# A mask add on GpSimd, split from one instruction of 1024 columns into two of 512

## The chip, the core and the metric

The kernel runs on one core of a Trainium2 chip. The metric is device time in microseconds (us) from launch to end, over repeated runs; smaller is better. A separate profiled execution gives the trace that all readings here come from. Engine names: PE is the matrix engine, DVE the vector engine, ACT the scalar engine, POOL is GpSimd, SP the engine that issues the DMAs.

## The reference, cut to what matters

The input is 64 graphs of 256 nodes with 512 features each, an adjacency matrix per graph and a node mask. Four layers follow each other; each normalises the rows (layer norm, then maximum with zero), runs a graph layer and adds its result to `x`. The change lies in layer 1, an attention over neighbours with 8 heads:

```python
dense = e_self[..., :, None] + e_neigh[..., None, :]
dense = jax.nn.leaky_relu(dense, negative_slope=0.2)
dense = dense + NEG_BIG * (1.0 - A[:, None, :, :])
att = jax.nn.softmax(dense, axis=-1)
```

The third line is the neighbour mask: -1e10 is added wherever two nodes aren't joined. Layers 0 and 3 weigh nodes by a softmax over one number per node, layer 2 uses `tanh` of masked scores.

## The kernel before, in words

**Tiling.** A graph's rows lie on 128 partitions, two rows to a partition (`NC` = 2). All data is float32. Buffers come from pools of one size each: `big` (1024 columns), `mid` (512 columns), `bank` (PSUM, 512 columns).

**Order.** Each graph is a set of named steps. A table of times (`TIMES`, with other tables for the first and the last graphs) says when each step of each graph is due; `Plan.run` sorts all steps of all 64 graphs by due time and records their instructions in that order. Every instruction is tied to the one before it on its engine, so the order on each engine is fixed, and an engine never overtakes a waiting instruction. Several graphs are in flight at once: while graph b is in layer 1, graph b+1 is in layer 0 and older graphs are in layers 2 and 3. DMAs are all issued by SP, in order.

**The steps around the change.** Heads are handled in four pairs p = 0 to 3, each in one `big` tile `e{p}` of 2 heads x 2 x 256 columns:

- `ea{p}` (line 1445, ACT): four Prelu instructions of 256 columns, two per head, fill the tile.
- `eg{p}` (line 1452, POOL): the mask `negt` (512 columns, the same for both heads) is added to the whole tile.
- `eb{p}` (line 1458, DVE): the row maximum is subtracted.
- `ex{p}` (line 1464, ACT): exponential. `po{p}` (line 1476, PE): product with the features. `eh{p}` (line 1487, POOL): sum of the two column halves.

On POOL, in the steady part of the run, the order of one turn of the loop is: `add3` of an old graph (line 1722, two instructions), `eg2`, `eg3`, the four sums of a Strassen-like product (`xsa` and `xsb`, lines 1172, 1173, 1179, 1180, which read rows brought by a gather DMA of line 1017), `eg0`, then a normalisation (lines 1092, 1097, 1098), `eg1`, and further sums, normalisations and `eh` steps.

On DVE, in the same stretch: sixteen max reductions (line 1407), then `mxv`, four small instructions of 128x16 (lines 1418, 1420, 1421, 1422) that turn the row maxima into the value to subtract, `mxt` (line 1427), then for the next graph the scores of layer 0 (`s0v`, line 1312), transposes and the softmax (line 1136), four scaled additions (`add0`, line 1325) and the sum of the row sums (`ms1`, line 1333). PE waits for `s0v` at its transposes of line 1131. ACT waits for `ms1` at line 1082, POOL then computes the scale (lines 1092 to 1098), ACT normalises (line 1103), and after that comes the first exponential (line 1464) for which PE waits at line 1476.

Of the kernel before, what the change touches and what calls it, by code (L numbers as in the profile page):

```python
# [11 lines left out]
OP = mybir.AluOpType  # L12
# [4 lines left out]
P = 128  # L17
D = 512
KC = D // P
N = 256  # L20
NC = N // P
# [705 lines left out]
class Graph:  # L727
# [5 lines left out]
    def step(self, name):  # L733
        def add(run):
            self.steps[name] = run
            return run
        return add
# [21 lines left out]
def tile_four_gnn_layers(ctx: ExitStack, tc: tile.TileContext, x, adj, nodemask,  # L759
# [6 lines left out]
    nc = tc.nc  # L766
# [253 lines left out]
    def graph(b):  # L1020

        g = Graph(plan)
# [415 lines left out]
        def attention(p):  # L1438
            @step(f"ea{p}")
            def _():  # L1440
                e = g.take("pair", 2, name=f"e{p}")
                for s in range(2):
                    h = 2 * p + s
                    for j in range(NC):
                        nc.scalar.activation(e[:, s, j, :], g[f"s{h // HA}"][:, h % HA, :], AF.Prelu,  # L1445
                                             bias=st["ec"][:, j, H + h:H + h + 1], alpha=0.2)
                g.done(f"s{p // 2}")

            @step(f"eg{p}")
            def _():  # L1450
                e = g[f"e{p}"]
                nc.gpsimd.tensor_tensor(e, e, g["negt"][:, None].to_broadcast([P, 2, NC, N]), OP.add)  # L1452
                g.done("negt")

            @step(f"eb{p}")
            def _():
                e = g[f"e{p}"]
                nc.vector.tensor_tensor(e, e, g[f"m{p // 2}"][:, p % 2 * 2:p % 2 * 2 + 2, None, :].to_broadcast([P, 2, NC, N]),  # L1458
                                        OP.subtract)
                g.done(f"m{p // 2}")  # L1460

            @step(f"ex{p}")
            def _():
                nc.scalar.activation(g[f"e{p}"], g[f"e{p}"], AF.Exp)  # L1464


            @step(f"po{p}")
            def _():
                e, q = g[f"e{p}"], p // 2
                if p % 2 == 0:  # L1470
                    g.take("bank", name=f"o{q}")
                po = g[f"o{q}"].rearrange("p (r n) -> p r n", r=2)
                for j in range(NC):
                    for s in range(2):
                        h = 2 * p + s
                        nc.tensor.matmul(po[s * U:(s + 1) * U, p % 2, :],  # L1476
                                         g[f"feats{j}"][:, E + h * U:E + (h + 1) * U],
                                         e[:, s, j, :], start=(j == 0), stop=(j == NC - 1))
                g.done(f"e{p}")
                for j in range(NC):  # L1480
                    g.done(f"feats{j}")


            @step(f"eh{p}")
            def _():
                e = g[f"e{p}"]
                nc.gpsimd.tensor_tensor(g.take("half", name=f"h{p}"), e[:, :, 0, :], e[:, :, 1, :], OP.add)  # L1487
                g.done(f"e{p}")
# [273 lines left out]
```

## Time and profile before

| what | us |
|---|---|
| median of 3 runs (lowest, highest) | 3696.07 (3695.48, 3696.09) |
| profiled execution, its own time | 3695.02 |
| its span, first to last instruction | 3693.2 |
| PE busy | 3401.5 (92%) |
| DVE busy | 3314.2 (90%) |
| ACT busy | 2781.7 (75%) |
| POOL busy | 2270.6 (61%) |
| POOL, line 1452: 256 instructions, mean 2.370 | 604.0 |
| POOL idle just before line 1452 | 98.6 |

A line of the profile names the source line, the engine, the operation, what is written and read, the shape and the count; behind the bar stand the busy time, the mean length of one instruction in ns, and the idle time of the engine just before it with what ended it. A line of the timeline starts with the time from the start of the span and the length, both in us; square brackets hold the idle time before it. Consecutive equal instructions are merged ("x2").

### The profile page before, as it was taken

The page shows a single profiled execution, that of the slowest core. Times are in us where ns is not written, and L with a number is a line of the kernel's source. Part 1 is how long each engine was busy: PE and PEld are TensorE (multiplying, and loading weights), DVE is VectorE, ACT ScalarE, POOL GpSimd, SP SyncE. Part 2 cuts the span into 40 slices and gives each one's busy share as a digit, 9 for nine tenths or more (in the row PEclk, how much of TensorE's full clock was granted, in tenths as well). Part 3 has the DMA queues.
Part 4 walks back from the last instruction along what each step waited for, and adds up shares of the span by engine and source line. Part 5 has one row for each costly group of instructions (what it writes and reads, how often), then busy time and mean ns, then how long its engine had stood idle before and what let it go on. Part 6 is the DMA issues. An engine that isn't in the chain of part 4 may idle for free.

```text
span 3693.2 us, 61427 instructions
## 1 busy us (share of the span) xinstructions
PE 3401.5 (92%) x16834; PEld 2175.5 (59%) x16834; DVE 3314.2 (90%) x8248; ACT 2781.7 (75%) x6533; POOL 2270.6 (61%) x2452
## 2 busy tenths in 40 slices
PE   5688999999999999999999999999999999989988
PEld 3455655665665666666666666666666666556554
DVE  6789998999999999999999989999989999999985
ACT  3667777787787787787778778778878778778765
POOL 3565665666666666666666666666666666565653
PEclk8799999999999999999999999999999999999999
DMA  6666766777777777777777777777777777767663
GB/s 185 181 188 208 207 213 212 222 220 216 222 219 218 222 222 217 225 224 224 227 215 221 226 216 217 230 222 219 226 216 219 223 219 221 217 204 216 197 190 119
DMA packets 995143, 785.28 MB, mean 213 GB/s; under 512 B 791984, under 2 KB 862192, under 8 KB 994800
## 3 DMA queue, kind: packets, MB, share of 16 engines
q1 hardware_dynamic: 994800, 781.35, 70.3%
q8 instruction: 137, 2.24, 0.2%
q14 instruction: 206, 1.69, 0.1%
HBM read 511.12 MB, written 270.01 MB: 212 GB/s over the span
## 4 chain that ended last, share of the span: by engine, by line
POOL 22%; DVE 18%; issue 15%; PE 14%; DMA 12%; ACT 7%; SPq 6%; POOLq 0%; ACTq 0%; DVEq 0%
PE bank L1188 9%; DMA big<-sq_d 8%; SPq L1017 5%; DVE big L1458 4%; DVE junk L1407 3%; POOL big L1452 3%; POOL rstd L1092 3%; POOL mid L1487 3%; POOL big L1173 3%; DMA sq_d<-big 3%; POOL big L1172 2%; POOL big L1179 2%; DVE big L1202 2%; DVE big L1012 2%; ACT big L1082 2%
## 5 line engine op out<-in xcount | busy, mean ns | idle before, releaser
L1188 PE MATMUL bank<-t_s,big 128*128 128x264 f32 (+3 forms) x3072 | 978.0, 452 | 8.3 <-DVE big L1657 6.1
L1188 PE MATMUL bank<-w_s,big 128*128 128x264 f32 (+2 forms) x3072 | 850.9, 410 | 45.9 <-DMA big<-sq_d 36.3
L1188 PEld LDWEIGHTS bank<-t_s,big 128*128 128x128 f32 x3072 | 583.0, 194 | 306.5 <-issue 180.5
L1188 PEld LDWEIGHTS bank<-w_s,big 128*128 128x128 f32 x3072 | 583.8, 196 | 278.5 <-issue 131.8
L1452 POOL TENSOR_TENSOR big<-big,mid 128x1024 f32<-128x1024 f32 x256 | 604.0, 2370 | 98.6 <-ACT big L1445 89.0
L1012 DVE STREAM_TRANSPOSE big<-big 128x512 f32<-128x512 f32 x640 | 483.6, 782 | 143.6 <-ACT big L1103 143.5
L1092 POOL TENSOR_TENSOR rstd<-rstd,power 128x2 f32<-128x2 f32 x256 | 183.9, 718 | 678.8 <-ACT rstd L1088 628.2
L1103 ACT ACTIVATE big<-big,shift,rstd 128x512 f32<-128x512 f32 x512 | 387.7, 805 | 167.3 <-POOL shift L1098 167.0
L1172 POOL TENSOR_TENSOR big<-big 128x256 f32<-128x256 f32 x256 | 226.6, 885 | 412.9 <-DMA big<-sq_d 278.7
L1487 POOL TENSOR_TENSOR mid<-big 128x512 f32<-128x512 f32 x256 | 377.1, 1493 | 138.2 <-ACT big L1464 138.2
L1407 DVE CUSTOM_DVE_ANT_0 junk<-big,bank 128x256 f32<-128x256 f32 x1024 | 428.9, 419 | 35.3 <-DMA big<-er_d 4.1
L1082 ACT ACTIVATE big<-big,sum 128x512 f32<-128x512 f32 x512 | 363.8, 712 | 116.7 <-DVE sum L1333 83.7
L1445 ACT ACTIVATE big<-big,ec 128x256 f32<-128x256 f32 x1024 | 428.8, 496 | 5.4 <-DMA big<-er_d 3.1
L1202 DVE TENSOR_TENSOR big<-bank,big 128x320 f32<-128x320 f32 (+1 forms) x704 | 399.5, 571 | 18.2 <-PE bank L1188 13.7
L1476 PE MATMUL bank<-big,big 128*64 128x256 f32 x2048 | 260.7, 388 | 92.2 <-ACT big L1464 91.9
L1458 DVE TENSOR_TENSOR big<-big,big 128x1024 f32<-128x1024 f32 x256 | 325.2, 1309 | 6.5 <-DMA big<-m_d 6.5
L1633 PE MATMUL bank<-big,big 64*128 64x256 f32 x2048 | 283.8, 398 | 50.5 <-DVE mx L1407 31.4
L1657 DVE TENSOR_TENSOR big<-bank,mid 128x512 f32<-128x512 f32 x512 | 319.9, 677 | 5.3 <-PE bank L1633 5.2
L1664 ACT ACTIVATE big<-big 128x512 f32<-128x512 f32 x512 | 293.1, 619 | 14.3 <-DVE big L1657 12.3
L1464 ACT ACTIVATE big<-big 128x1024 f32<-128x1024 f32 x256 | 267.8, 1052 | 41.4 <-DVE big L1458 33.6
L1633 PEld LDWEIGHTS bank<-big,big 64*128 64x128 f32 x2048 | 219.7, 197 | 131.4 <-ACT big L1621 65.1
L1536 ACT ACTIVATE big<-big,rs 128x64 f32<-128x64 f32 x1024 | 257.4, 334 | 24.5 <-DVE rs L1525 13.2
(132 smaller groups left out, 5877.8 us busy)
## 6 DMA issues: line engine op xcount, KB each, us to landing
sq_d<-big SPq DMA_DIRECT2D x448, 512.0 KB
big<-sq_d SPq DMA_DIRECT2D x1792, 128.0 KB
big<-er_d SPq DMA_DIRECT2D x256, 512.0 KB
big<-m_d SPq DMA_DIRECT2D x128, 512.0 KB
big<-in_x_dram SPq DMA_DIRECT2D x64, 512.0 KB
out_dram<-big SPq DMA_DIRECT2D x64, 512.0 KB
mid<-in_adj_dram SPq DMA_DIRECT2D x64, 256.0 KB
mid<-in_adj_dram SPq DMA_DIRECT2D x256, 64.0 KB
```

The costliest lines, as they stand in the source:

```text
L1012: nc.vector.transpose(sq.rearrange("p (r k i c) -> p c k r i", r=4, k=KC, c=NC)[:, c], t[:, c])
L1082: nc.scalar.activation(g["hn"][:, c, :], g["xt"][:, c, :], AF.Square, scale=-float(D), bias=st["sum"][:, c:c + 1], accum_out=st["ssq"][:, ...
L1103: nc.scalar.activation(g["hn"][:, c, :], g["xt"][:, c, :], AF.Relu, bias=st["shift"][:, c:c + 1], scale=st["rstd"][:, c:c + 1])
L1188: nc.tensor.matmul(p, a()[:, k], w[:, k], start=(k == 0), stop=(k == 1))
L1202: nc.vector.tensor_tensor(out(), g[i][:, :w], old(), OP.add)
L1407: nc.vector.tensor_tensor_reduce(junk, g[f"n{h // HA}"][:, h % HA, :], g["far"][:, c * N:(c + 1) * N], 1.0, -BIG, OP.add, OP.max, g["mx"][ ...
L1445: nc.scalar.activation(e[:, s, j, :], g[f"s{h // HA}"][:, h % HA, :], AF.Prelu, bias=st["ec"][:, j, H + h:H + h + 1], alpha=0.2)
L1452: nc.gpsimd.tensor_tensor(e, e, g["negt"][:, None].to_broadcast([P, 2, NC, N]), OP.add)
L1458: nc.vector.tensor_tensor(e, e, g[f"m{p // 2}"][:, p % 2 * 2:p % 2 * 2 + 2, None, :].to_broadcast([P, 2, NC, N]), OP.subtract)
L1487: nc.gpsimd.tensor_tensor(g.take("half", name=f"h{p}"), e[:, :, 0, :], e[:, :, 1, :], OP.add)
L1633: nc.tensor.matmul(ps[s][:, m, :], chunk(g["xpt"][half, p], m), g["xc"][half, p, :], start=True, stop=True)
L1657: nc.vector.tensor_tensor(th[:, s], g[f"ps{p}{s}"].rearrange("p (m n) -> p m n", m=NC), g["at"], OP.mult)
```

## The change

`eg{p}` loops over the two heads of a pair and adds the mask to each head's 512 columns in an instruction of its own. The broadcast of the mask over the heads goes away, since each instruction reads the mask once. The order of the steps, the other engines' instructions and all buffers stay as they are.

```diff
             @step(f"eg{p}")
             def _():
                 e = g[f"e{p}"]
-                nc.gpsimd.tensor_tensor(e, e, g["negt"][:, None].to_broadcast([P, 2, NC, N]), OP.add)
+                for s in range(2):
+                    nc.gpsimd.tensor_tensor(e[:, s], e[:, s], g["negt"], OP.add)
                 g.done("negt")
```

## The prediction

> **What bounds the kernel.** I first read busy shares: PE 92%, DVE 90%, POOL only 61%. So POOL's work matters only through what it makes others wait for. Next, PE's waits in the steady part (697 to 3115 us, 44 turns of the loop, one graph leaving per turn; mean turn 54.95 us):
>
> ```profile
> PE bank L1476 <- ACT big L1464: 60.1, 44, 2.5
> PE bank L1131 <- DVE bank L1312: 39.8, 43, 2.0
> PE bank L1633 <- DVE mx L1407: 24.6, 44, 1.0
> ```
>
> These 124 us (2.8 us per turn) are nearly all of PE's idle time there. Two of three end on DVE, so I read DVE's timeline in one turn, then POOL's over the same microseconds:
>
> ```profile
> 1853.06 0.92 DVE L1418 TENSOR_TENSOR mx<-mx,ec 128x16 f32<-128x16 f32 x1
> 1854.02 0.83 DVE L1420 TENSOR_SCALAR mx<-mx 128x16 f32<-128x16 f32 x1
> 1854.88 0.17 DVE L1421 SCALAR_TENSOR_TENSOR mx<-mx 128x16 f32<-128x16 f32 x1
> 1855.09 0.59 DVE L1422 TENSOR_TENSOR mx<-mx 128x16 f32<-128x16 f32 x1
> ...
> 1855.88 0.20 DVE L1312 SCALAR_TENSOR_TENSOR bank<-bank,big 128x64 f32<-128x64 f32 x1
> ```
>
> ```profile
> 1845.90 2.51 POOL L1722 TENSOR_TENSOR big<-big,big 128x512 f32<-128x512 f32 x2
> 1849.28 4.68 POOL L1452 TENSOR_TENSOR big<-big,mid 128x1024 f32<-128x1024 f32 x2 [0.86 <-ACT big L1445]
> 1853.97 0.85 POOL L1172 TENSOR_TENSOR big<-big 128x256 f32<-128x256 f32 x1
> 1854.89 0.75 POOL L1173 TENSOR_TENSOR big<-big,big 128x256 f32<-128x256 f32 x1
> ```
>
> Four equal small DVE instructions take 0.17 or up to 0.92 us. L1418 ends at 1853.98, 0.02 after `eg3` (1853.96); L1420 at 1854.85, when L1172 ends (1854.82); L1422 at 1855.68, when L1173 ends (1855.64). DVE stands still until the running POOL instruction is over. The path: `eg2`, `eg3` on POOL hold `mxv`; `mxv` holds `s0v` (L1312); PE waits for it at L1131; DVE, without a gap, goes on to `add0` and `ms1`, from which ACT, POOL and ACT again lead to the exponential PE waits for at L1476. In 41 of 42 steady turns that wait ends 6.90 to 6.92 us after `ms1` starts, and a straight line through turn length against `ms1`'s place has slope 1.3: what `ms1` gains, the turn gains.
>
> The trace holds one turn in which the pair happened to start early:
>
> ```profile
> 2618.74 4.67 POOL L1452 TENSOR_TENSOR big<-big,mid 128x1024 f32<-128x1024 f32 x2 [0.86 <-ACT big L1445]
> ...
> 2623.06 0.39 DVE L1418 TENSOR_TENSOR mx<-mx,ec 128x16 f32<-128x16 f32 x1
> 2623.48 0.17 DVE L1420 TENSOR_SCALAR mx<-mx 128x16 f32<-128x16 f32 x1
> 2623.69 0.17 DVE L1421 SCALAR_TENSOR_TENSOR mx<-mx 128x16 f32<-128x16 f32 x1
> 2623.90 0.18 DVE L1422 TENSOR_TENSOR mx<-mx 128x16 f32<-128x16 f32 x1
> 2624.11 0.25 DVE L1427 STREAM_TRANSPOSE mr<-mx 128x64 f32<-128x64 f32 x1
> 2624.28 0.20 DVE L1312 SCALAR_TENSOR_TENSOR bank<-bank,big 128x64 f32<-128x64 f32 x1
> ```
>
> L1312 comes 1.22 us after L1418, against 2.82 above. That turn lasted 53.3 us, one of the shortest.
>
> **What the Trainium skill says.** "SBUF — State Buffer", section "Who interferes with whom": DVE and GpSimd share one port pair, "an exclusive lock"; a DVE instruction with two SBUF inputs, or in a 2-port mode such as `tensor_scalar` may enter, blocks for the whole of a GpSimd instruction that reads SBUF, and the other way round. The trace agrees: the ends above, and POOL's 128x2 L1097, 1.18 us under a DVE L1458 instead of 0.20. "Perfetto Trace Analysis", section "GPSIMD Engine Instruction", advises timing GpSimd by start-to-start spacing; I do.
>
> **The change, part by part.**
>
> *Length.* Start to start, `eg2` to `eg3` takes 2.32 us for 1024 columns. The nearest row for 512 is L1722, same operation on float32: 1.24 (2.51 for two, 1.28 the last). An `eg` thus grows by 2 x 1.24 - 2.32 = 0.16 us; 256 of them add 41 us to POOL. Bounds: 0.1 (half is the true floor, plus little) to 0.25 (an extra wait instruction, 0.02 each in the trace, and dispatch). This lies in POOL's idle time (39%): after `eg0` POOL idles 4.6 us per turn for ACT, after `eg1` 2.3. Without that cover it would cost up to 41 us.
>
> *Start.* The old instruction waits for all four Prelus. In the built program the first half waits only for its head's second Prelu. ACT runs the eight Prelus of `ea2`, `ea3` in 3.29 us, 0.41 each, so it may start 0.82 us earlier, at 1848.46; POOL is free at 1848.41. It uses nearly all of its 0.86 us of idle time; later halves wait for nothing. End of `eg3`: 1848.46 + 3 x 1.24 + 1.28 = 1853.46, against 1853.96: 0.50 earlier.
>
> *What follows.* L1418 is let go at about 1853.49. Where L1172 isn't running yet, L1420 to L1422 then take 0.17 each and `s0v` comes 1.2 us after L1418's start. L1172's start is set by its gather's landing, which SP issues after `store`, behind L1722, so it doesn't move. Two things cap the gain at L1325 (`add0`). ACT: it idles 0.97 us before L1141 in this turn, and L1325 starts 0.26 after it may, so 1.23 at most. POOL: L1325 has two SBUF inputs and can now arrive while `eg0`, 0.16 longer, still runs. In late turns it already does:
>
> ```profile
> 2023.80 2.37 POOL L1452 TENSOR_TENSOR big<-big,mid 128x1024 f32<-128x1024 f32 x1
> ...
> 2025.84 0.55 DVE L1325 SCALAR_TENSOR_TENSOR big<-big,w,big 128x192 f32<-128x192 f32 x1
> ```
>
> L1325 ended 0.22 after `eg0` instead of 0.40 after its start; there the change costs 0.15. I read all 44 turns by the gather's landing after L1418's start: up to 1.0 us, 21 turns, gains 0.7 to 1.24, mean 0.95; 1.0 to 1.4, 10 turns, `eg0`'s new end binds, mean 0.64; above, 13 turns, -0.1. Sum 20.0 + 6.4 - 1.3 = 25 us, 0.57 per turn. PE's two waits (2.3 us per turn together) have room for it.
>
> *`eg1`.* It ends 0.16 later, and `eb0` on DVE starts just at its end (L1458 at 1869.00, `eg1` ends 1869.09). The delay passes to the exponentials; PE needs the last about 0.2 us after it is done, and DVE next idles for PE at L1270. Taken as nothing; without that cover, 0.16 x 64 = 10 us.
>
> *Head and tail* (20 turns): L1418 takes 17.1 us there, single stalls reaching 2.4 us, which halves would shorten, but PE waits more for ACT and DMA. I take 0.3 each, 6 us (bounds 0 and 15).
>
> Total -31 us on the profiled 3695.02: 3664, and the median stands 1 us above: 3665.
>
> **Rivals.**
> 1. *Half of it* (0.20): another wait soon takes over: PE at L1633, ACT, or more turns with late gathers. About 0.25 per turn: -15 us, 3681. For: 13 turns gain nothing already.
> 2. *More* (0.12): late turns gain too, since DVE may enter between the halves of `eg0`; 0.9 per turn plus ends: -52 us, 3644. Against: the second half then blocks the next L1325.
> 3. *Slower* (0.07): the early start doesn't come about, and `eg3` ends 4 x 1.24 - 2 x 2.32 = 0.32 later, straight onto L1418. 0.32 x 44 plus `eg0`'s and `eg1`'s 0.16: about +20 us, 3716. It decides once the start moves by less than 0.32 us. Against: the waits in the built program.
> 4. *No difference* (0.06): DVE isn't the path, or the pair's gain is given back at `eg0`: 3696.
>
> My forecast has 0.55. Below 0.2% (7.4 us) a measurement of this kernel can't tell a change from none. Faster: 0.55 + 0.20 + 0.12 = 0.87; same 0.06; slower 0.07. The range, 3642 to 3689, takes in rivals 1 and 2 and leaves 3 and 4 out.
>
> **What would show it.** L1452's successor: 512 instructions of about 1.28 us, POOL busy up about 41. The first half of `eg2` starts within 0.1 us of L1722's end. L1418's mean falls from 0.95 to about 0.45 us, L1420 to L1422 mostly 0.17. PE's wait at L1131 halves in the steady part, that at L1476 stays near 1.3 per turn or drops when PE becomes the bound; the turn falls from 54.95 to 54.4. L1325 is stalled more often, up to `eg0`'s end. I am wrong if L1418 shortens but the turn doesn't (PE or another chain bounds), or if `eg3` ends no earlier.

## The result and the profile after

| | before | after |
|---|---|---|
| median, us (lowest, highest), 4 runs each | 3695.78 (3692.9, 3696.09) | 3662.64 (3661.1, 3665.39) |
| profiled execution, own time, us | 3695.02 | 3662.73 |
| its span, us | 3693.2 | 3660.9 |

The changed kernel takes 0.9913 of the time before, 95% interval 0.9896 to 0.993: 33 us faster, or 26 to 38. The forecast was 31 us faster (3665).

The page's first part and its row for the split mask add, after the change (what follows line 1452 has moved down by one line: 1464 is now 1465, 1476 is 1477, 1633 is 1634, 1722 is 1723):

```profile
PE 3404.0 (93%) x16834; PEld 2175.1 (59%) x16834; DVE 3278.9 (90%) x8248; ACT 2780.4 (76%) x6533; POOL 2313.9 (63%) x2708
...
L1453 POOL TENSOR_TENSOR big<-big,mid 128x512 f32<-128x512 f32 x512 | 649.0, 1294 | 42.9 <-ACT big L1445 33.0
```

POOL is busy 43 us longer (2270.6 before) and the kernel is 33 us faster. DVE is busy 35 us less (3314.2 before), though not one of its instructions was edited: it stands still less. PE does the same work in the same time (3401.5 before).

PE's waits over the 44 steady turns, after (releaser, us in total, times, longest):

```profile
PE bank L1477 <- ACT big L1465: 68.5, 44, 2.4
PE bank L1634 <- DVE mx L1407: 21.3, 41, 0.9
PE bank L1131 <- DVE bank L1312: 8.7, 16, 1.2
```

Before, these were 60.1, 24.6 and 39.8. The wait at L1131 has lost 31.1 us, the one for the exponential has gained 8.4, the one at L1634 has lost 3.3: 26 us less. The steady part, measured from the 12th to the 56th L1418, went from 2418.5 to 2392.3 us, 26.2 less. Over just that stretch all of PE's idle time fell from 124.6 to 99.8 us and its busy time by 1.3, so PE's idle time tells nearly the whole of it. A turn takes 54.37 us instead of 54.97.

One steady turn after the change, POOL's timeline and then DVE's (start, length, idle time before in brackets):

```profile
1994.86 2.52 POOL L1723 TENSOR_TENSOR big<-big,big 128x512 f32<-128x512 f32 x2
1997.43 4.97 POOL L1453 TENSOR_TENSOR big<-big,mid 128x512 f32<-128x512 f32 x4
2002.97 0.85 POOL L1172 TENSOR_TENSOR big<-big 128x256 f32<-128x256 f32 x1 [0.57 <-DMA big<-sq_d]
```

```profile
2001.98 0.45 DVE L1418 TENSOR_TENSOR mx<-mx,ec 128x16 f32<-128x16 f32 x1
2002.47 0.17 DVE L1420 TENSOR_SCALAR mx<-mx 128x16 f32<-128x16 f32 x1
2002.68 0.17 DVE L1421 SCALAR_TENSOR_TENSOR mx<-mx 128x16 f32<-128x16 f32 x1
2002.89 0.17 DVE L1422 TENSOR_TENSOR mx<-mx 128x16 f32<-128x16 f32 x1
2003.10 0.25 DVE L1427 STREAM_TRANSPOSE mr<-mx 128x64 f32<-128x64 f32 x1
2003.27 0.20 DVE L1312 SCALAR_TENSOR_TENSOR bank<-bank,big 128x64 f32<-128x64 f32 x1
```

The old 0.86 us of idle time ahead of `eg2` is gone: the four halves follow L1723 after 0.05 us. They end at 2002.40, L1418 at 2002.43, and then POOL idles for its gather: L1420 and L1421 run in that gap, L1422 starts just ahead of L1172, and all three take 0.17. L1312 starts 1.29 us after L1418 does (2.82 in the turn shown before). In the same turn on PE:

```profile
2004.05 0.43 PE L1131 MATMUL bank<-ident,wc 128*128 128x128 f32 x2
...
2016.89 1.08 PE L1477 MATMUL bank<-big,big 128*64 128x256 f32 x8 [1.44 <-ACT big L1465]
```

There is no bracket at L1131 any more: `s0v` is there before PE is. The wait that is left is the one for the exponential.

### The profile page after: what moved, and what is told of

It reads as the page before. It is cut to its first block, busy times and chain, and to the rows that moved or that the text cites. A ratio compares the mean times of both kernels' runs of the same rounds, so it can differ in the third digit from the quotient of the medians.

```text
span 3660.9 us, 61887 instructions
## 1 busy us (share of the span) xinstructions
PE 3404.0 (93%) x16834; PEld 2175.1 (59%) x16834; DVE 3278.9 (90%) x8248; ACT 2780.4 (76%) x6533; POOL 2313.9 (63%) x2708
## 4 chain that ended last, share of the span: by engine, by line
DVE 20%; PE 19%; POOL 18%; issue 13%; DMA 11%; ACT 7%; SPq 5%; POOLq 0%; ACTq 0%; DVEq 0%
PE bank L1188 13%; DMA big<-sq_d 6%; SPq L1017 4%; DVE junk L1407 4%; DVE big L1459 3%; POOL big L1453 3%; DVE big L1202 3%; PE bank L1477 3%; DVE big L1012 2%; POOL rstd L1092 2%; POOL big L1173 2%; POOL big L1172 2%; DMA sq_d<-big 2%; POOL big L1179 2%; POOL mid L1488 2%
## 5 line engine op out<-in xcount | busy, mean ns | idle before, releaser
L1188 PE MATMUL bank<-t_s,big 128*128 128x264 f32 (+3 forms) x3072 | 978.9, 452 | 8.0 <-DVE big L1658 5.7
L1188 PE MATMUL bank<-w_s,big 128*128 128x264 f32 (+2 forms) x3072 | 847.1, 409 | 44.5 <-DMA big<-sq_d 35.7
L1188 PEld LDWEIGHTS bank<-t_s,big 128*128 128x128 f32 x3072 | 582.0, 193 | 308.2 <-issue 176.7
L1188 PEld LDWEIGHTS bank<-w_s,big 128*128 128x128 f32 x3072 | 582.1, 195 | 273.9 <-issue 131.0
L1453 POOL TENSOR_TENSOR big<-big,mid 128x512 f32<-128x512 f32 x512 | 649.0, 1294 | 42.9 <-ACT big L1445 33.0
L1092 POOL TENSOR_TENSOR rstd<-rstd,power 128x2 f32<-128x2 f32 x256 | 183.6, 717 | 641.0 <-ACT rstd L1088 584.3
L1172 POOL TENSOR_TENSOR big<-big 128x256 f32<-128x256 f32 x256 | 226.6, 885 | 437.3 <-DMA big<-sq_d 288.1
L1477 PE MATMUL bank<-big,big 128*64 128x256 f32 x2048 | 261.6, 390 | 103.8 <-ACT big L1465 99.4
L1634 PE MATMUL bank<-big,big 64*128 64x256 f32 x2048 | 286.0, 400 | 45.9 <-DVE mx L1407 27.4
L1634 PEld LDWEIGHTS bank<-big,big 64*128 64x128 f32 x2048 | 221.6, 198 | 127.4 <-ACT big L1622 58.7
```

What stands on the lines that cost most here:

```text
L1188: nc.tensor.matmul(p, a()[:, k], w[:, k], start=(k == 0), stop=(k == 1))
L1453: nc.gpsimd.tensor_tensor(e[:, s], e[:, s], g["negt"], OP.add)
L1477: nc.tensor.matmul(po[s * U:(s + 1) * U, p % 2, :], g[f"feats{j}"][:, E + h * U:E + (h + 1) * U], e[:, s, j, :], start=(j == 0), stop=(j = ...
L1634: nc.tensor.matmul(ps[s][:, m, :], chunk(g["xpt"][half, p], m), g["xc"][half, p, :], start=True, stop=True)
```

## The experiments

All are compared with the kernel before, run beside them; intervals are 95%.

**The halves in the other order.** The second head's half waits for all four Prelus, so the early start is taken away and the two short instructions kept. The diff is against the changed kernel.

```diff
-                for s in range(2):
+                for s in (1, 0):
                     nc.gpsimd.tensor_tensor(e[:, s], e[:, s], g["negt"], OP.add)
```

> Both halves stay, but head 1 goes first, so the first half waits for all four Prelus as the old instruction did. My theory (the gain is the earlier start, which makes eg3 end earlier and frees L1418): eg3 now ends 4 x 1.24 - 2 x 2.32 = 0.32 us later than before, L1418 grows by about 0.3 us, the steady turn grows by 0.2 to 0.5 us, the time is 3703 to 3718 (before: 3695.8). Rival (shorter instructions let DVE in sooner, and that alone is worth it): most of the gain stays, 3665 to 3685.

Measured: 3710.56 us against 3694.33, ratio 1.0047 (1.0034 to 1.006). POOL and DVE in a steady turn of this kernel:

```profile
1845.77 2.51 POOL L1723 TENSOR_TENSOR big<-big,big 128x512 f32<-128x512 f32 x2
1849.14 4.97 POOL L1453 TENSOR_TENSOR big<-big,mid 128x512 f32<-128x512 f32 x4 [0.86 <-ACT big L1445]
1854.12 0.85 POOL L1172 TENSOR_TENSOR big<-big 128x256 f32<-128x256 f32 x1
```

```profile
1852.91 1.23 DVE L1418 TENSOR_TENSOR mx<-mx,ec 128x16 f32<-128x16 f32 x1
1854.17 0.82 DVE L1420 TENSOR_SCALAR mx<-mx 128x16 f32<-128x16 f32 x1
...
1855.24 0.60 DVE L1422 TENSOR_TENSOR mx<-mx 128x16 f32<-128x16 f32 x1
```

And PE's waits in its steady part:

```profile
PE bank L1131 <- DVE bank L1312: 60.5, 45, 1.7
PE bank L1477 <- ACT big L1465: 47.3, 36, 1.8
PE bank L1634 <- DVE mx L1407: 23.6, 41, 0.9
```

The gap of 0.86 us ahead of `eg2` is back, and the four halves take 0.29 more than the 4.68 of two whole instructions: L1418 is held to 1854.14 and L1420 falls under L1172 again. This is the third rival of the prediction, "slower", made to happen: it was 3716 there, and 3711 here. PE's wait at L1131 rises by 21 us, and that for the exponential gives 13 of them back. The steady part is still 20 us longer: 7 by the three waits together, 7 by PE's clock (27.3 us at half rate against 13.2, of which half is lost), and 6 that I can't assign. Short instructions alone gain nothing; the gain needs the earlier start.

**Only pairs 2 and 3, only pair 2, only pairs 0 and 1.** The same edit with three lists of pairs, (2, 3), (2,) and (0, 1); the diff shows the first, against the changed kernel:

```diff
+                if p in (2, 3):
                     for s in range(2):
                         nc.gpsimd.tensor_tensor(e[:, s], e[:, s], g["negt"], OP.add)
+                else:
+                    nc.gpsimd.tensor_tensor(e, e, g["negt"][:, None].to_broadcast([P, 2, NC, N]), OP.add)
```

> Only eg2 and eg3 are split; eg0 and eg1 are one instruction of 1024 columns again. My theory: the early start and the earlier end of eg3 stay, and eg0 ends 0.16 us sooner, which frees L1325 in those turns (some 27 of 44) where it waits for eg0: about 0.1 us per turn better than the full split, 3656 to 3661. Rival (the split of eg0 and eg1 carries a good part of the gain, since DVE may enter between their halves): 3668 to 3685.

> Only eg2 is split. My theory: only the first instruction of the pair had anything to win by an early start, so eg3 as one instruction ends another 0.16 us sooner (at 0.25 us after L1418's start, against 0.41 with the full split); eg0 also is 0.16 shorter. 3650 to 3660, the fastest of these. Rival (eg3's split is needed, because it also waits for Prelus or because DVE enters between its halves): slower than the split of both, 3665 to 3690.

> Only eg0 and eg1 are split; eg2 and eg3 are as before. My theory: no gain in the steady turns, a loss of up to 0.16 us where L1325 waits for eg0 (some 13 of 44 turns): 3694 to 3702. Rival (finer instructions help wherever DVE meets them): 3670 to 3688.

| pairs split | median, us | ratio (interval) | steady turn, us | L1418, mean ns, steady |
|---|---|---|---|---|
| 2 and 3 | 3654.95 | 0.9895 (0.9881 to 0.9908) | 54.24 | 527 |
| 2 | 3653.47 | 0.9898 (0.9884 to 0.9911) | 54.11 | 344 |
| 0 and 1 | 3696.82 | 1.0012 (1.0003 to 1.002) | 55.07 | 1019 |

Pair 2 alone and pairs 0 and 1 lie where the theory expected them; pairs 2 and 3 are 1 us below its range. That pair 2 alone is the fastest isn't shown: by the ratios the first two rows are alike. POOL's timeline with pair 2 alone split:

```profile
1824.10 2.52 POOL L1726 TENSOR_TENSOR big<-big,big 128x512 f32<-128x512 f32 x2
1826.67 2.51 POOL L1454 TENSOR_TENSOR big<-big,mid 128x512 f32<-128x512 f32 x2
1829.14 2.37 POOL L1456 TENSOR_TENSOR big<-big,mid 128x1024 f32<-128x1024 f32 x1
1832.37 0.85 POOL L1172 TENSOR_TENSOR big<-big 128x256 f32<-128x256 f32 x1 [0.87 <-DMA big<-sq_d]
```

From `eg2`'s start to `eg3`'s end it is 4.84 us here and 4.97 with both split. PE's waits in the steady part with pairs 0 and 1 alone split:

```profile
PE bank L1480 <- ACT big L1468: 59.6, 44, 2.0
PE bank L1131 <- DVE bank L1312: 44.2, 42, 1.8
PE bank L1637 <- DVE mx L1407: 20.2, 40, 0.9
```

Splitting `eg2` alone is enough for the whole gain. Splitting `eg0` and `eg1` costs 0.12%, 4 us (1 to 7), less than the 0.2% that the prediction took as the least a measurement can tell. With fewer pairs split the ratios are lower than the full split's by 0.0015 to 0.0018, some 6 us; the intervals overlap, so this much is likely and not shown, and whether splitting `eg3` does harm isn't resolved at all.

**`eg3` ends earlier without a split or an early start.** `eg2` adds the mask to one head alone, in one instruction of 512 columns; the mask is missing for head 0 of pair 2.

```diff
-                nc.gpsimd.tensor_tensor(e, e, g["negt"][:, None].to_broadcast([P, 2, NC, N]), OP.add)
+                if p == 2:
+                    nc.gpsimd.tensor_tensor(e[:, 1], e[:, 1], g["negt"], OP.add)
+                else:
+                    nc.gpsimd.tensor_tensor(e, e, g["negt"][:, None].to_broadcast([P, 2, NC, N]), OP.add)
```

> The kernel before, with one piece of work left out: eg2 adds the mask to head 1 alone, so the mask is missing for head 0 of pair 2. No instruction is split and none starts earlier, but eg3 ends some 0.74 us sooner (it then waits for its own Prelus). My theory (what counts is when eg3 ends): L1418 falls to about 0.2 us, and the gain is that of splitting eg2 alone, 3645 to 3660. Rival (the early start helps in another way, as by a smoother ACT or PE): little gain, 3680 to 3696.

Measured: 3638.97 us against 3698.27, ratio 0.9842 (0.9819 to 0.9865). The rival is out by far, and the theory's range is missed by 6 us. POOL in a steady turn of this kernel:

```profile
1819.05 1.27 POOL L1453 TENSOR_TENSOR big<-big,mid 128x512 f32<-128x512 f32 x1 [0.86 <-ACT big L1445]
1820.64 2.36 POOL L1455 TENSOR_TENSOR big<-big,mid 128x1024 f32<-128x1024 f32 x1 [0.32 <-ACT big L1445]
1823.89 0.85 POOL L1172 TENSOR_TENSOR big<-big 128x256 f32<-128x256 f32 x1 [0.89 <-DMA big<-sq_d]
```

`eg2` starts after its usual 0.86 us of idle time, and from that start to `eg3`'s end it is 3.95 us instead of 4.68, so the end comes 0.73 earlier. With pair 2 alone split, it comes 0.82 - 0.16 = 0.66 earlier. The two steady turns agree as the two ends do, 54.06 and 54.11 us: what counts is when `eg3` ends, by whatever means. The miss lies outside the steady part. Against the kernel with pair 2 split, the profiled head is 5.2 us shorter and the tail 7.9, where the expectation had nothing; POOL has 1.2 us less to do per graph, but which wait that shortens I did not follow up.

**`eg3` ends 1.35 us later.** In addition to the whole instruction, `eg2` adds the mask to head 1 once more. From `eg2`'s start to `eg3`'s end it is then 6.03 us instead of 4.68.

```diff
                 nc.gpsimd.tensor_tensor(e, e, g["negt"][:, None].to_broadcast([P, 2, NC, N]), OP.add)
+                if p == 2:
+                    nc.gpsimd.tensor_tensor(e[:, 1], e[:, 1], g["negt"], OP.add)
```

> The kernel before, with a third instruction of 512 columns in eg2 that adds the mask to head 1 once more. eg3 ends 1.3 us later. My theory: L1418 stalls for about 2.2 us, the gathers have landed by then so that L1420 and L1422 are held too, and the steady turn grows by 1.3 to 1.9 us: 3750 to 3785. Rival (PE bounds, and the DVE stall is only in part on the path): less than half of that, 3700 to 3725.

Measured: 3821.91 us, ratio 1.0341 (1.0311 to 1.0371). The direction is right, but the time is 37 us above the range of the theory. PE's timeline in a turn of this kernel:

```profile
1913.60 0.43 PE L1131 MATMUL bank<-ident,wc 128*128 128x128 f32 x2 [2.58 <-DVE bank L1312]
1913.95 3.21 PE L1188 MATMUL bank<-w_s,big 128*128 128x264 f32 x8
1916.95 1.57 PE L1188 MATMUL bank<-t_s,big 128*128 128x256 f32 x4
```

The same stretch by busy time (us of PE, weight load, DVE, ACT, POOL with counts; then the granted PE clock, the DMA share, GB/s):

```profile
1913.60:1916.00 2.40, 2.40 (x8) 1.88 (x9) 2.40 (x6) 0.55 (x3) 2.40 (x2) 0.71 0.07 19
1916.00:1918.00 2.00, 2.00 (x6) 1.53 (x5) 2.00 (x6) 2.00 (x7) 0.32 (x1) 0.50 1.04 371
```

PE waits 2.58 us for `s0v`, and then its granted clock falls to half for a few microseconds: eight matmuls take 3.21 us. In the kernel before, a wait of 2.00 us at the same place was not followed by this:

```profile
1912.17 0.43 PE L1131 MATMUL bank<-ident,wc 128*128 128x128 f32 x2 [2.00 <-DVE bank L1312]
1912.51 2.02 PE L1188 MATMUL bank<-w_s,big 128*128 128x264 f32 x8
```

In the lengthened kernel's steady part PE ran at half rate for 129.7 us, in 38 of 44 turns, against 13.2 us before. In these stretches one 128x256 matmul of L1188 follows another after 427 ns instead of 216, so work takes twice as long, and this adds (129.7 - 13.2) / 2 = 58 us. The steady part grew by 114.7 (2418.5 to 2533.2): PE's busy time by 69, with these 58 in it, and its idle time by 46.

The turns tell the two parts from each other. The 6 in which the clock stayed at full last 56.35 us on average, 1.39 more than before, within the 1.3 to 1.9 of the theory. The 38 others last 57.77, 2.80 more. In both kinds `ms1` comes 1.6 us later after L1418's start than before. But the wait for the exponential, which in 43 of 44 turns before ends 6.9 us after `ms1` starts, ends 6.9 after it in those 6 and 7.9 in those 38. DVE and POOL in the turn shown:

```profile
1921.36 2.48 DVE L1659 TENSOR_TENSOR big<-bank,mid 128x512 f32<-128x512 f32 x4 [1.35 <-PE bank L1635]
1923.77 2.52 DVE L1460 TENSOR_TENSOR big<-big,big 128x1024 f32<-128x1024 f32 x1
```

```profile
1922.83 2.37 POOL L1452 TENSOR_TENSOR big<-big,mid 128x1024 f32<-128x1024 f32 x1
```

The slow PE keeps DVE waiting, so `eb2` (L1460, 1.22 us unhindered) comes late, falls under `eg1` (L1452), and the exponential falls behind with it; in the steady part `eb2` takes over 2 us, and L1659 waits over 0.5 us for PE, in just these 38 turns. So the delay passes to the turn in full, and the slow clock, with the second hold that it brings, doubles the bill. The theory had no term for that: it is what its range missed.

**The next wait.** With pair 2 alone split, L1477's wait for the exponential (L1480 in that kernel) is what remains:

```profile
PE bank L1480 <- ACT big L1468: 69.8, 44, 2.3
```

On the way to it POOL computes the scale. POOL and DVE in a turn of that kernel:

```profile
1841.35 0.70 POOL L1092 TENSOR_TENSOR rstd<-rstd,power 128x2 f32<-128x2 f32 x1 [3.70 <-ACT rstd L1088]
1842.13 1.18 POOL L1097 TENSOR_TENSOR shift<-sum,rstd 128x2 f32<-128x2 f32 x1
1843.38 0.19 POOL L1098 TENSOR_TENSOR shift<-shift,share_of 128x2 f32<-128x2 f32 x1
```

```profile
1839.65 2.47 DVE L1661 TENSOR_TENSOR big<-bank,mid 128x512 f32<-128x512 f32 x4
1842.04 1.22 DVE L1462 TENSOR_TENSOR big<-big,big 128x1024 f32<-128x1024 f32 x1
```

`eb2` (L1462, two SBUF inputs) starts just ahead of L1097 and holds it for its whole length. The edit moves `eb2` ahead of the last two products L1661, so that L1092 starts under it instead (the diff is against the kernel with pair 2 alone split):

```diff
-... "eb2": 43.450, "ex2": 43.459,
+... "eb2": 43.150, "ex2": 43.459,
```

> Only eg2 is split, and in the steady turns eb2 (DVE, 1024 columns, two SBUF inputs) is due one step earlier, ahead of the last two products with the adjacency. In the traces so far eb2 starts just before POOL's L1097 and holds it for 1.0 us on the path to PE's wait at the exponential. My theory (the hold works in both directions, and this one is on the path): L1097 falls to 0.2 us; POOL's L1092, which now starts while eb2 runs, is held some 0.6 us instead; so the turn gains 0.3 to 0.5 us, 3630 to 3645, against 3653 with eg2 split alone. Rival (ACT or PE bounds this stretch, or eb2 then waits for the row maxima to land): within 5 us of 3653, or slower.

Measured: 3637.27 us against 3696.83, ratio 0.9837 (0.982 to 0.9854); the turn fell from 54.11 to 53.61 us. POOL in a turn of this kernel:

```profile
1882.45 1.27 POOL L1092 TENSOR_TENSOR rstd<-rstd,power 128x2 f32<-128x2 f32 x1 [4.04 <-ACT rstd L1088]
1883.80 0.20 POOL L1097 TENSOR_TENSOR shift<-sum,rstd 128x2 f32<-128x2 f32 x1
```

PE's waits in its steady part:

```profile
PE bank L1480 <- ACT big L1468: 50.2, 44, 2.1
PE bank L1637 <- DVE mx L1407: 21.7, 41, 1.1
PE bank L1131 <- DVE bank L1312: 4.4, 10, 1.0
```

From L1092's start to L1097's end it was 1.96 us and is 1.55: L1092 is now held, but only partly, and L1097 not at all. This is the gain: the wait for the exponential ended 6.91 us after `ms1` starts and now ends 6.49 after it (medians of 44 turns). PE's wait for the exponential falls by 19.6 us, of 21.6 that the steady part gains in these two traces. This kernel computes the reference in full and is the fastest of those that do, ahead of both the kernel before and the changed one, whose interval (0.9896 to 0.993) lies wholly above.

## Why the prediction was right, by its steps

**Length: right.** 512 instructions of 1.29 us, POOL busy 43 us longer where 41 were said, and nearly all of it stayed in POOL's idle time (pairs 0 and 1, half of the added work, cost 4 us). The Trainium skill's page "SBUF — State Buffer", section "Who interferes with whom", calls the shared ports an exclusive lock; the lines after agree, as L1418 ends 0.03 us after `eg3`.

**Start: right.** The first half starts 0.05 us after L1723 in the turn shown, within the 0.1 that was said, and over the steady part `eg3` ends 5.03 us after L1723 does, where it was 5.54 after L1722 (medians): 0.51 earlier, where 0.50 was said. With the halves in the other order this start, and the gain with it, went away.

**What follows: right in sum, with two of its waits read wrongly.** 25 us were said for the 44 turns, 26.2 were measured, 0.60 per turn against 0.57. The path is the one named: the wait for the exponential ends 6.9 us after `ms1` starts in 43 of 44 turns before and in all 44 after. In part the sum is luck: after L1418's start `ms1` comes 0.69 us sooner (9.05 to 8.36), more than the 0.57 said, and the rest of the turn is 0.09 longer, where nothing was said. L1418's steady mean went from 0.98 to 0.54 us (0.45 said), L1420 to L1422 from 0.41, 0.29 and 0.40 to 0.18, 0.19 and 0.30. The cap at L1325 is there, too. In a turn with a late gather, POOL and DVE after the change:

```profile
1950.31 2.52 POOL L1453 TENSOR_TENSOR big<-big,mid 128x512 f32<-128x512 f32 x2
```

```profile
1951.80 1.25 DVE L1325 SCALAR_TENSOR_TENSOR big<-big,w,big 128x192 f32<-128x192 f32 x1
```

L1325 is held to 1953.05, 0.22 after `eg0` ends (1952.83).

What failed is the sentence on PE's waits under "What would show it". L1131's wait was to halve and fell by almost four fifths; the one for the exponential was to stay or drop and rose from 1.37 to 1.56 us per turn. Both misses have one reading: `s0v` gains more than `ms1` does. After L1418's start `s0v` comes 0.88 us sooner and `ms1` 0.69, so 0.20 is lost between them. PE is let go earlier at L1131, comes to the exponential earlier than the exponential does, and waits there for the difference, 0.19 per turn. Of the 0.20, 0.09 is the first L1325, held longer on average (0.52 to 0.60 us), as by `eg0` in the lines above; the rest is lost on DVE before L1325 starts, and I did not follow up to what. The prediction had sized the turn's gain by `ms1`, which was the right choice.

**`eg1` as nothing: a little too low.** `eg0` and `eg1` together cost 4 us (1 to 7) when split alone. That is less than the 10 us named for `eg1` without cover, so most of its delay is hidden. The single traces show some of it: with the full split `ms1` comes as soon as with pairs 2 and 3 alone (8.36 us after L1418's start in both), but from there to the next L1418, where `eg1` lies, the turn is 0.13 us longer; with pairs 0 and 1 alone this stretch is 0.04 longer than before. That would be 2 to 6 us, and isn't more exact than that.

**Head and tail: right in sum.** 6 us were said; the profiled head is 2.5 us shorter and the tail 3.6. Between the kernels of this study, these parts differ by several us in ways that I can't assign, so part of this agreement may be chance.

**The rivals.** "Slower" has its mechanism confirmed by the reversed order, and it didn't occur since the start did come early. "More" is not what the split did. A gain of its size, 0.86 us per turn, came with pair 2 alone split, and so without any halves of `eg0` for DVE to enter between. Another wait did take over, as in "half of it", but only 8.4 us of it.

## What to carry to other kernels

An instruction on a lightly used engine can cost its length on another engine that is locked out while it runs: look for small equal instructions whose lengths vary, and see which instruction's end theirs coincide with. Split only the instruction that an input really delays (here `eg2`, one of four; splitting the others gained nothing that these runs show), and put first the half whose input comes first; in the other order the split loses. Then look for the same lock in the other direction: moving one DVE instruction ahead of two others was worth another 22 us of the steady part.

## What the runs showed that I had not expected

**PE's clock answers to waits much shorter than I had thought.** The Trainium skill, "TensorE: Matmul & The Clock Gate", section "Part 1: The HAM clock gate", has the clock at half rate after an idle window of about 3.4 us. Here less was enough, and the measurement decides. In the seven traces with any stretch at half rate in their steady part, all these stretches start and end on one grid of 3.413 us per trace, within 0.01 us. So I cut the steady parts of all nine traces into the cells of their grids and took the cells at full clock. In 43 of them PE was idle for 2.0 us or more, and the clock fell at the end of every one; with 1.9 to 2.0 us it fell after 10 of 14, with less after 10 of 6232 (eight of these with the halves in the other order, at 1.55 to 1.7 us, for a reason I don't know). Each stretch lasted 3.41 us, which costs 1.7 us of matmul time. A wait on PE that grows to about 2 us can thus have a price beyond its own length, if enough of it falls into one cell. Of the 2.58 us shown above 2.39 lie in one cell; the 2.00 us of the kernel before are cut by the grid, with about 1.1 us idle in each of two cells, and no fall followed.

**A held instruction gets in between two GpSimd instructions that follow each other without a gap.** In the lines with the halves in the other order, the last half ends at 1854.11 and L1172 starts at 1854.12; L1418, waiting since 1852.91, ends at 1854.14, and L1172 takes its usual 0.85. L1420, next, is held again, to the end of L1172. In that kernel's steady part 21 of 41 held L1418 end like this, 0.03 to 0.04 us after `eg3`, with L1172 following without a gap. So with POOL busy without a break, each small DVE instruction pays for the rest of one POOL instruction, not for the whole row of them. Of the longer L1325, which ended 0.22 us after its holder and takes 0.40 unhindered, part of the work must overlap the hold.
